# SS2D scan: VectorE instead of GpSimd makes the fourth product u in groups 3 and 6 of a step

## The chip, the cores and the metric

The kernel runs on one core of one Trainium2 chip. Its engines are TensorE (PE; its weight loads are listed as PEld), VectorE (DVE), ScalarE (ACT), GpSimd (POOL) and SyncE (SP), which issues the DMAs. Each engine works through its own queue in order; semaphores hold an instruction until what it needs is there. The metric is the device time of one execution in microseconds (us), lower is better.

## The reference, cut to what matters

The network has four layers on 8 images of 56 x 56 positions with 128 channels. Layers 0, 2 and 3 are deformable convolutions; layer 1 is a visual state space block (VSS), and the change lies in its scan ("SS2D"). Cut to that:

```python
xb = silu(dwconv3x3(in_proj(layer_norm(x))) + conv_b)         # 256 channels
xs = [x0, x1, reversed x0, reversed x1]                        # rows, columns, both ways
dts, B, C = split(x_proj_k @ xs_k)                             # for each direction k
dt = softplus(dt_proj_k @ dts + dt_bias_k)
def step(h, t):                                                # over the 3136 positions
    h = h * exp(dt_t * A) + (dt_t * u_t) * B_t                 # 256 channels x 16 states
    y = sum_n(h * C_t)
y = sum over the 4 directions of (y_k + Ds * xs_k)
x = x + out_proj(layer_norm(y) * silu(z));  x = x + mlp(layer_norm(x))
```

The state h has 256 x 16 = 4096 rows for each direction. The scan is linear in h, and the same for all rows, so that rows can stand in the 128 partitions and positions along the free axis.

## The kernel before, in words

The function `scans` of class `Vss` runs 128 *steps*: 8 images x 4 directions (in the order 1, 3, 0, 2) x 4 chunks of 784 positions. A step has 32 *units*: 8 *groups* cg of 32 channels, and in each group 4 scans sg of 4 states; a unit is 128 rows (32 channels x 4 states) x 784 positions. "Scan 3.2" is here scan sg=2 of group cg=3. For each unit:

- ScalarE makes dA = exp(A dt) into PSUM (`decay`, L1369; two buffers), so dA of a unit waits for the scan two units before.
- The product u = (dt x) B is made (`inputs`). For scans 0, 1 and 2 of a group VectorE makes it (L1379) from dtu, a copy of dt x in PSUM, and b; the tile u has two buffers. For scan 3 GpSimd makes it (L1375) from dt in SBUF and b; the tile is called up and has one buffer. GpSimd cannot read PSUM.
- VectorE scans (L1471): h = dA * h + u along the positions; h has three buffers, so a scan waits for the hc of three units before. ScalarE keeps the last column in st (L1474).
- GpSimd multiplies hc = h C (L1476); six buffers.
- TensorE adds hc over the states into acc (`add_sums`, L1401, two units at a time); ScalarE copies acc out after two groups (`close_sums`, L1412).

dtu of a group is a product of dt with the identity on TensorE (`spread`, L1363; four matmul rows, one buffer, so the spread of the next group waits for the last u that reads this one). dt of a group is fetched two groups ahead by SP (`fetch_dt`, L1314), b and c rows near the end of a step (`fetch_row`, L1307).

Beside this, `prepare` makes dt, dt x, B and C of the next step in pieces, one piece in each of scans 1 and 2 of every group. Its pieces for GpSimd are a sum (L1294) and a product (L1296) for each half of the channels; by program order they fall into groups 3 and 6. An output stage (layer norm, gate, projection, MLP; L1194 to L1252) and the next image's input stage (layer norm, 3x3 convolution as nine matmuls, SiLU) run as tasks that `advance` takes one piece of in scans 1, 2 and 3 of a group. The MLP takes fc1 (L1235), its bias on ScalarE (L1236), a Gelu (L1238) with a table load ahead of it and one back to the exp table (L1240), and fc2 with its bias row (L298, L1245, L1247).

Program order is not queue order. Every `tile` belongs to a pool with a number of buffers, and a scheduler sets the order of each engine's queue at build time: it takes instructions by priority (program order) as its own estimate of times makes them ready. So an instruction that becomes ready earlier or later in that estimate can move on its queue past others of independent work.

Of the kernel before, what the change touches and what calls it, by code (L numbers as in the profile page):

```python
# [133 lines left out]
NCG, NSG = DI // TC, NST // TS  # L134
# [855 lines left out]
class Vss:  # L990
# [332 lines left out]
    def scans(self):  # L1323
# [5 lines left out]
        order = [(cg, sg) for cg in range(NCG) for sg in range(NSG)]  # L1329
# [23 lines left out]

        def on_pool(t):

            return order[t][1] == NSG - 1

        def spread(at, t):

# [11 lines left out]
        def inputs(at, t):  # L1371
            s, (cg, sg) = state[at], order[t]
            if on_pool(t):
                u = self.work.tile([128, SC], F32, name="up", tag="up", bufs=1)
                nc.gpsimd.tensor_mul(u, s["dt", cg][:, 1], s["b", sg])  # L1375
            else:
                u = self.work.tile([128, SC], F32, name="u", tag="u", bufs=2)
                halves = [v.rearrange("p (x e) -> p x e", x=2) for v in (u, s["b", sg])]
                nc.vector.tensor_mul(halves[0], s["dtu", cg][:, :, :SH], halves[1])  # L1379
            s["u", t] = u  # L1380
# [47 lines left out]
        for now, (at, t) in enumerate(units):  # L1428
# [28 lines left out]
            if now + 1 < len(units):  # L1457
                decay(*units[now + 1])
                if not on_pool(units[now + 1][1]):
                    inputs(*units[now + 1])  # L1460

                if sg == NSG - 3 and now + 3 < len(units):
                    spread(*units[now + 3])
            if now + 2 < len(units) and on_pool(units[now + 2][1]):
                inputs(*units[now + 2])
# [100 lines left out]
```

## Time and profile before

| what | value |
|---|---|
| times of three runs | 18138.38, 18144.38, 18144.70 us (median 18144.38) |
| profiled execution | 18131.72 us |
| its span, first to last instruction | 18130.2 us, mean granted TensorE clock 0.849 |
| DVE, POOL, ACT, PE busy | 15374.0, 11790.9, 10917.1, 13876.0 us |
| scans, L1471, from u and from up | 3072 of 1838 ns, 1024 of 1833 ns |
| u on VectorE, L1379 | 3072 of 955 ns |
| up on GpSimd, L1375 | 1024 of 1860 ns |
| hc on GpSimd, L1476 | 4096 of 1877 ns |
| sum and product of the preparation, L1294, L1296 | 254 each in the scan stage, of 1862 and 2055 ns |
| spread, L1363 | 4096 matmul rows of 622 ns, four to a spread |

Busy time counts an instruction from its start to its end; neighbours on one engine overlap by some 0.1 us, so that the distance from start to start is a little shorter than the duration (two u in a row take 1.83 us). "Idle before, releaser" is the time that an engine stood still ahead of an instruction and what ended it. A wait view sums these by waiting line and releaser. In the timeline, equal neighbours stand in one row with their count.

### The profile page before, as it was taken

Reading aid. Unit: us, or ns where it says so; the run is one execution under the profiler, and the core shown is the slowest. Engines: PE = TensorE matmul, PEld = TensorE weight load, DVE = VectorE, ACT = ScalarE, POOL = GpSimd, SP = SyncE. Lnnn points to the kernel's source line nnn. Section 1 sums busy time; section 2 is a strip of 40 time slices with the busy share of each in tenths; the row PEclk is TensorE's granted clock in tenths of the full one; section 3 lists DMA queues with packets and bytes.
Section 4 is the critical chain, followed back from the end, with each engine's and each line's share of the span. In section 5 each row is a group of like instructions: output and inputs, shape, how many; then the busy total and the mean of one; then the engine's idle time right before and its main releaser. Section 6 shows DMA issues by size and latency. Waiting matters only on the chain. (4 is left out here: it accounts for less than half of the span.)

```text
span 18130.2 us, 255599 instructions
## 1 busy us (share of the span) xinstructions
PE 13876.0 (77%) x90059; PEld 6901.9 (38%) x90059; DVE 15374.0 (85%) x17784; ACT 10917.1 (60%) x19602; POOL 11790.9 (65%) x6462
## 2 busy tenths in 40 slices
PE   5777787688688688688788778778676888577777
PEld 4655422233232232232223223222134666455555
DVE  8888368998998998998998898899976887688886
ACT  4666555566566566566566566656554666456666
POOL 2221079998998998998998998999971111222221
PEclk7778888899899899899899899889886888677777
DMA  7777444444443443444443444444335777577777
GB/s 216 210 200 206 133 146 157 160 170 154 146 158 139 143 160 137 147 157 142 141 159 139 148 156 141 143 156 149 138 120 141 198 199 197 148 203 202 203 200 174
DMA packets 1341766, 2961.81 MB, mean 163 GB/s; under 512 B 91168, under 2 KB 892132, under 8 KB 1325836
## 3 DMA queue, kind: packets, MB, share of 16 engines
q1 hardware_dynamic: 1340460, 2945.21, 52.4%
q8 instruction: 720, 11.80, 0.3%
q14 instruction: 586, 4.80, 0.1%
HBM read 2243.88 MB, written 866.92 MB: 172 GB/s over the span
## 5 line engine op out<-in xcount | busy, mean ns | idle before, releaser
L1476 POOL TENSOR_TENSOR hc<-h,c 128x784 f32<-128x784 f32 x4096 | 7559.1, 1877 | 594.7 <-DVE h L1471 348.4
L1471 DVE TENSOR_TENSOR_SCAN h<-dA,st,u 128x784 f32<-128x784 f32 x3072 | 5572.7, 1838 | 367.1 <-ACT dA L1369 190.2
L1369 ACT ACTIVATE dA<-dt,v_A 128x784 f32<-128x784 f32 x4096 | 3743.1, 915 | 864.5 <-DVE h L1471 852.9
L1401 PE MATMUL acc<-hc,v_sum 128*32 128x392 f32 x16384 | 3105.8, 533 | 141.4 <-POOL hc L1476 139.8
L1379 DVE TENSOR_TENSOR u<-dtu,b 128x784 f32<-128x784 f32 x3072 | 2860.7, 955 | 398.8 <-PE dtu L1363 390.7
L1363 PE MATMUL dtu<-dt,ident 128*128 128x392 f32 x4096 | 2012.8, 622 | 1221.8 <-issue 864.5
L736 POOL TENSOR_TENSOR ay<-hat,om 112x756 f32<-112x756 f32 (+2 forms) x192 | 516.2, 2688 | 2755.4 <-ACT hat L727 2359.4
L1471 DVE TENSOR_TENSOR_SCAN h<-dA,st,up 128x784 f32<-128x784 f32 x1024 | 1877.2, 1833 | 297.0 <-POOL hc L1476 278.1
L1375 POOL TENSOR_TENSOR up<-dt,b 128x784 f32<-128x784 f32 x1024 | 1904.6, 1860 | 65.9 <-DVE h L1471 33.4
L807 ACT COPY st<-pt 128x448 f32<-128x448 f32 (+1 forms) x2240 | 1175.8, 541 | 1218.2 <-PE pt L805 1211.3
L1474 ACT COPY st<-h 128x1 f32<-128x1 f32 x3072 | 583.5, 190 | 2047.5 <-DVE h L1471 2040.5
L775 DVE TENSOR_TENSOR win<-win,patch 112x252 f32 (+2 forms) x3456 | 1691.7, 502 | 125.8 <-DVE win L775 33.1
L805 PE MATMUL pt<-ident,sw 112*128 112x112 f32 (+2 forms) x8960 | 1609.8, 310 | 208.2 <-DMA sw<-skew 208.1
L1401 PEld LDWEIGHTS acc<-hc,v_sum 128*32 128x32 f32 x16384 | 758.1, 115 | 2547.2 <-issue 1630.8
L1363 PEld LDWEIGHTS dtu<-dt,ident 128*128 128x128 f32 x4096 | 848.3, 227 | 2251.6 <-issue 1348.9
L766 POOL MEMSET win<- 128x1820 f32 (+2 forms) x384 | 630.4, 1648 | 1461.4 <-DMA skew<-win 1156.3
L821 PE MATMUL yps<-st,xw 128*32 128x48 f32 (+5 forms) x35840 | 1076.4, 245 | 399.1 <-ACT st L807 396.3
L805 PEld LDWEIGHTS pt<-ident,sw 112*128 112x128 f32 (+2 forms) x8960 | 1119.5, 161 | 493.3 <-DMA sw<-skew 169.7
L772 DVE TENSOR_TENSOR patch<-ay,hat 112x756 f32<-112x756 f32 (+2 forms) x1152 | 1222.1, 1066 | 20.9 <-POOL ay L736 17.9
L821 PEld LDWEIGHTS yps<-st,xw 128*32 128x32 f32 (+2 forms) x35840 | 755.4, 125 | 827.2 <-ACT st L807 475.9
L725 ACT ACTIVATE hat<-om,taps 112x252 f32<-112x252 f32 x1280 | 755.7, 729 | 287.5 <-DVE patch L772 270.2
L1128 PE MATMUL misc<-xn,v_tap 128*128 128x448 f32 x2016 | 837.4, 563 | 64.0 <-ACT xn L1162 27.2
(193 smaller groups left out, 19611.3 us busy)
## 6 DMA issues: line engine op xcount, KB each, us to landing
dt<-dds SPq DMA_DIRECT2D x1024, 784.0 KB
b<-rows SPq DMA_DIRECT2D x512, 392.0 KB
c<-rows SPq DMA_DIRECT2D x512, 392.0 KB
dds<-dd SPq DMA_DIRECT2D x256, 784.0 KB
sw<-skew SPq DMA_DIRECT2D x224, 812.0 KB
sw<-skew SPq DMA_DIRECT2D x224, 672.0 KB
sw<-skew SPq DMA_DIRECT2D x224, 588.0 KB
xw<-table SPq DMA_DIRECT2D x224, 320.0 KB
```

Source lines behind the costliest of these rows:

```text
L772: nc.vector.tensor_mul(patch[:n], bcast(a, 3, KX), bcast(b, 2, KY))
L775: self.last_add = nc.vector.tensor_add(to, to, patch[:n, NCB * p : NCB * (p + 1)]).ins
L805: last = nc.tensor.transpose(ps[:m, n * g : n * (g + 1)], sw[:n, g, p : p + m], self.net.ident[:n, :n])
L807: nc.scalar.copy(st[:m], ps[:m, : G * n])
L821: self.nc.tensor.matmul(yps[CG * g : CG * (g + 1), t0:t1], lhsT=xw[:m, k + part, CG * g : CG * (g + 1)], rhs=st[:m, at + t0 : at + t1], st ...
L1363: last = nc.tensor.matmul(ps[:, b, :SH], lhsT=self.net.ident, rhs=s["dt", cg][:, 1, SH * b : SH * (b + 1)], start=True, stop=True)
L1369: nc.scalar.activation(da[:, :SC], s["dt", cg][:, 0], AF.Exp, scale=w["A"][:, k, NSG * cg + sg : NSG * cg + sg + 1])
L1375: nc.gpsimd.tensor_mul(u, s["dt", cg][:, 1], s["b", sg])
L1379: nc.vector.tensor_mul(halves[0], s["dtu", cg][:, :, :SH], halves[1])
L1401: nc.tensor.matmul(acc[r : r + TC, :SH], lhsT=w["sum"], rhs=hc[:, SH * b : SH * (b + 1)], start=False, stop=sg == NSG - 1)
L1471: nc.vector.tensor_tensor_scan(hh[:, ::step], dA[:, :SC][:, ::step], u[:, ::step], st[:, t : t + 1], ALU.mult, ALU.add)
L1476: nc.gpsimd.tensor_mul(hc, hh, s["c", sg])
```

## The change: which u GpSimd makes

In groups 3 and 6 VectorE makes all four products u, scan 3 included, from dtu; there GpSimd makes none. In the other six groups nothing is different: scan 3's product is GpSimd's. So 256 of the 1024 up become u (2 in each of 128 steps), and the scans 3.3 and 6.3 read u instead of up.

```diff
         def on_pool(t):
 
-            return order[t][1] == NSG - 1
+            cg, sg = order[t]
+            return sg == NSG - 1 and cg not in (3, 6)
```

`on_pool` is asked in `inputs`, and in the loop over units: up is asked for two units ahead of its scan (L1464 to L1465), u one unit ahead (L1459 to L1460). The spread of the next group stands in the program after the u of scan 2 and, in groups 3 and 6 of the changed kernel, ahead of the u of scan 3; since both use the one buffer of dtu, that spread waits for this u.

## The prediction

> **What bounds the kernel now.** First the page: VectorE (DVE) is busy 85% of the span, GpSimd (POOL) 65%, but the page's slices show that GpSimd does nearly all of its work in the stage where both stand at 8 to 9 tenths, the SS2D scans. The first scan starts at 2363 us, the last ends at 13501 us: 128 steps, 11138 us, 87.0 us a step. All that the change touches lies in there.
>
> ```profile
> span 18130.2 us, 255599 instructions
> PE 13876.0 (77%) x90059; PEld 6901.9 (38%) x90059; DVE 15374.0 (85%) x17784; ACT 10917.1 (60%) x19602; POOL 11790.9 (65%) x6462
> ```
>
> Second, busy time by stretch, for three single steps. The columns are length, then busy time of PE, PEld, DVE, ACT, POOL, and the granted clock.
>
> ```profile
> 4815.53:4894.19 78.66, 41.76 (x176) 13.53 (x176) 77.60 (x57) 36.17 (x72) 73.22 (x42) 0.80 0.36 131
> 3831.00:3916.28 85.28, 73.68 (x277) 27.46 (x276) 79.61 (x58) 57.45 (x106) 82.32 (x46) 0.94 0.48 166
> 6047.60:6134.00 86.40, 60.48 (x205) 17.88 (x204) 78.43 (x58) 49.08 (x96) 86.40 (x48) 0.84 0.40 141
> ```
>
> The first step has none of the preparation on GpSimd: VectorE is never idle, and 78.7 us is its own work (32 scans, 24 products u). The second is the usual step with preparation; in the third GpSimd is busy all the time. So VectorE bounds, and what a step has over 78.7 is waits and a little stage work.
>
> Third, the waits of VectorE in the scan stage (waiting instruction, what it waited for, us in total, times, longest):
>
> ```profile
> DVE h L1471 <- POOL hc L1476: 341.2, 287, 3.3
> DVE u L1379 <- PE dtu L1363: 310.1, 130, 9.3
> DVE h L1471 <- ACT dA L1369: 195.5, 188, 5.0
> ```
>
> Placed by group and scan (group cg, scan sg), the 341 us lie: 72.3 at scan 3.3 and 72.2 at 6.3, the two that the change is about; the rest, by whole group 4, 5, 7, 0 and others, 54.4, 36.4, 72.4, 23.7 and about 10.
>
> Fourth, the timeline of group 3 in the step at 3831, VectorE and then GpSimd:
>
> ```profile
> 3863.30 0.97 DVE L1379 TENSOR_TENSOR u<-dtu,b 128x784 f32<-128x784 f32 x1
> 3864.19 3.58 DVE L1471 TENSOR_TENSOR_SCAN h<-dA,st,u 128x784 f32<-128x784 f32 x2
> 3869.69 1.85 DVE L1471 TENSOR_TENSOR_SCAN h<-dA,st,up 128x784 f32<-128x784 f32 x1 [1.92 <-POOL hc L1476]
> ```
>
> ```profile
> 3861.78 1.86 POOL L1375 TENSOR_TENSOR up<-dt,b 128x784 f32<-128x784 f32 x1
> 3863.59 1.89 POOL L1294 TENSOR_TENSOR dd<-dd,sp 128x784 f32<-128x784 f32 x1
> 3865.55 2.26 POOL L1296 TENSOR_TENSOR dd<-dd,xb 128x784 f32<-128x784 f32 x1
> 3867.76 7.38 POOL L1476 TENSOR_TENSOR hc<-h,c 128x784 f32<-128x784 f32 x4
> ```
>
> GpSimd runs product, sum and product in one piece before the first hc of the group. Three h buffers let scan 3.3 start only when hc 3.0 is done (3869.6): VectorE waits 1.92 us.
>
> **The change part by part.** (1) VectorE gets 256 more u (2 in each of 128 steps). Two u in a row take 1.83 us including overlap, one costs the queue 0.88: 256 x 0.875 = **+224 us**.
>
> (2) At 3.3 and 6.3 the new u runs inside the old wait. Wait by wait, the smaller of 0.875 and the wait adds to 45.2 + 46.4 = **-92 us**. The other waits right around them (a spread that TensorE delivers late for its own reasons, a late dA) hide more of it: counted the same way over scans 3.2 to 4.1 and 6.2 to 7.1, the cover is 80.7 + 63.4 = 144, so **-52 us** more. If that cover is gone, these 52 come back.
>
> (3) GpSimd loses 256 up of 1.86 us, but not where the text says. In the order of the built program, the place ahead of the sum and the product in group 3 is taken by group 4's up (it needs only dt, b and the single up buffer, and with up 3 gone that is free), and in group 6 by group 7's. The run of three before hc 3.0 stays, and the relief comes one group later. So scan 3.3 starts when it did. What can go is the hc waits of groups 4, 5, 7 and 0 and the rest at 6.3: 54.4 + 36.4 + 72.4 + 23.7 + 25.8 = 213. Bounds 0 and -213. I take rather over half, **-120**: in steps like the third above, where GpSimd is never idle, 48 operations become 45 and waits remain only around the runs of three. The early up 4 also wants dt 4 sooner: its 784 KB were issued at 3857.1, and at the 166 GB/s of that stretch take 4.7 us, about when up 4 would start (3861.8). A later landing would hold hc 3.0 behind it.
>
> (4) The spread (dtu, one buffer) of group 4 now waits for u 3.3 instead of u 3.2, so on TensorE's queue everything behind it (the sums over hc of groups 3) comes after that. What it costs VectorE depends on how many scans stand between the last u of a group and the first of the next. Over the whole stage, before: 0 scans 21 times, 1 scan 15, 2 or 3 scans 980; after: 50, 136 and 830. Prices from the trace: with 0 scans the gap is 2.79 us on average, as here:
>
> ```profile
> 4510.16 0.95 DVE L1379 TENSOR_TENSOR u<-dtu,b 128x784 f32<-128x784 f32 x1
> 4514.20 0.97 DVE L1379 TENSOR_TENSOR u<-dtu,b 128x784 f32<-128x784 f32 x1 [3.09 <-PE dtu L1363]
> ```
>
> with 1 scan 0.64 (16 places), with 2 scans 0.26. The 13 zeros at group 3 go, with the 41.4 us that stand at scan 3.2 for dtu: **-38**. The 121 new ones cost between 0 (a spread of 1.58 fits in a scan of 1.75) and 0.64 each, 77; the new ones stand mostly in steps with an undisturbed TensorE, so **+30**.
>
> (5) The 44 new zeros all stand at the end of a step, in the steps that run an output stage. There TensorE's queue changes: in 45 steps the next step's spread comes after the bias and first fc2 products, which need the Gelu; before, in none. And ScalarE now makes dA 7.2 after the Gelu and its two table loads. Rows of before:
>
> ```profile
> 3910.49 0.57 ACT L1236 ACTIVATE pre<-misc,v_col 128x392 f32<-128x392 f32 x1
> 3911.08 1.28 ACT L1238 ACT_TABLE_LOAD   x1
> 3912.37 1.51 ACT L1238 ACTIVATE pre<-pre 128x1568 f32<-128x1568 f32 x1
> ```
>
> ```profile
> 3910.43 1.58 PE L1363 MATMUL dtu<-dt,ident 128*128 128x392 f32 x4 [0.31 <-DVE u L1379]
> 3913.39 1.09 PE L298 MATMUL misc<-v_fc_b,ones 1*98 1x512 f32 x2
> ```
>
> From the start of scan 6.3: scan 1.85, st and dA 7.1 to 3.0, two copies of acc (0.90 each) to 4.8, the new acc 1.64 and sums 1.51 to 7.9 (the Gelu is done at 8.2, beside them), bias 1.09, x 0.3, fc2 0.5, spread 1.58: 11.4. Then u, two scans, u: next step's first scan at 16.7, where before it was 13.35 later (3902.93 to 3916.28): 3.35 more. In the steps of direction 2 the copies take 0.48 and acc 0.88, so 1.85. Mean 2.6 x 45 = **+117**; bounds 0 (the chain runs out early behind GpSimd's lead) and 45 x 3.35 = 150. The 44 further table loads of 1.28 us that ScalarE gets lie in this chain's shadow: 0, or up to 56 if not.
>
> SP's queue gets no other transfers, only some in another order: 0. TensorE and ScalarE compute the same: 0.
>
> Sum: 224 - 92 - 52 - 120 - 38 + 30 + 117 = **+69 us** on the profiled execution's 18131.7 (span 18130.2): 18201. The median of the three times, 18144.4, stands 12.7 higher: **18213 us**, 0.4% slower.
>
> One rule speaks against the change: the Trainium skill, Perfetto Trace Analysis, Identifying the Most-Contended Engine, says to improve the engine with the highest occupancy first. That would be VectorE, 77.60 of 78.66 us in the first stretch, and the change gives it more work: by the rule alone +224 us. The waits in the other two stretches say that part of this is hidden.
>
> **The rivals.** *Faster*: GpSimd's relief works in full, and the chain at the step's end is half hidden because GpSimd no longer lags there. 224 - 144 - 213 - 38 + 58 = -113: 18031. For it: the third stretch, where GpSimd is the bound outright. Against it: the run of three stays, and in the first stretch there is nothing to win. It decides if the hc waits fall below some 130 of 341 us. *Same*: relief a little larger than taken (-170) and the chain at 1.9 us (+85): -13, inside 0.2% (36 us), which is about what a measurement tells from no change. *The change does not do what it says*: the run of three keeps its length and relief is nil: 224 - 144 - 38 + 30 + 117 = +189: 18333. *Much slower*: nothing hides but the 92, all order costs at their top: 224 - 92 - 38 + 77 + 150 = +321: 18465.
>
> **How the numbers follow.** Forecast (from +36 to +190) 0.43, no relief or much slower 0.12, same 0.2, faster 0.25. So slower 0.55. The range leaves out a tenth at each end: below the faster rival's 18031 nearly, 18040, and above the no-relief case, 18335. The forecast's own range is 18180 to 18335.
>
> **What would show it.** Scans with u 3328, with up 768; the waits for hc at 3.3 fall by 0.9 each and do not vanish, those of groups 4, 5 and 7 shrink; waits of u for dtu grow at the end of 45 steps by some 2 us and vanish after u 3.2; the step without preparation takes 80.4 instead of 78.7. Wrong, if hc waits fall below 130 us (faster) or if u 0.0 after an output stage waits less than 1 us.

## The result, and the profile after

The changed kernel takes 18207.03 us (median of 7 runs, 18197.98 to 18216.24) where the kernel before takes 18144.70 on the same chip (7 runs, 18136.20 to 18157.83): ratio 1.0035, 95% interval 1.0026 to 1.0044. It is slower by 62 us; 18213 was predicted.

From the page of the changed kernel, span and busy time of each engine:

```profile
span 18205.5 us, 255708 instructions
PE 13892.2 (76%) x90059; PEld 6916.9 (38%) x90059; DVE 15561.4 (85%) x18040; ACT 11000.5 (60%) x19646; POOL 11341.0 (62%) x6206
```

DVE has 256 instructions more and POOL 256 fewer, as the change says. ACT has 44 more: all are table loads. The scan stage (start of the first scan to end of the last) went from 11137.8 to 11204.1 us, +66.3; what lies before and behind it differs by 0.6 and 8.4 us. So the loss is in the scan stage.

Busy time by stretch of the changed kernel, the same three steps as shown for before (columns: length, busy time of PE, PEld, DVE, ACT, POOL, granted clock, DMA share, GB/s):

```profile
4816.35:4896.33 79.98, 43.45 (x176) 13.99 (x176) 79.18 (x59) 36.16 (x72) 69.61 (x40) 0.81 0.36 126
3835.58:3924.40 88.82, 74.43 (x277) 27.42 (x276) 81.15 (x61) 59.34 (x106) 79.22 (x44) 0.92 0.48 162
6059.72:6144.11 84.39, 57.06 (x208) 17.79 (x208) 79.72 (x59) 51.81 (x100) 83.41 (x47) 0.84 0.43 155
```

Three kinds of step, three outcomes. The step without preparation went from 78.66 to 79.98: two u more, no wait to hide them. The step with preparation that ends in an output stage went from 85.28 to 88.82. The step in which GpSimd was busy without a break went from 86.40 to 84.39: there the change does what it looks like.

The waits of VectorE in the scan stage (waiting instruction, what it waited for, us in total, times, longest):

```profile
DVE u L1380 <- PE dtu L1364: 419.8, 213, 7.6
DVE h L1472 <- ACT dA L1370: 249.7, 179, 5.0
DVE h L1472 <- POOL hc L1477: 97.4, 128, 5.0
```

Before, these were 310.1 (dtu), 195.5 (dA) and 341.2 (hc). The wait for GpSimd fell by 244 us, more than the 212 (92 + 120) that the prediction took; the waits for TensorE and ScalarE rose by 110 and 54. Added up over the trace by place, the largest changes are (us, before to after): hc at scan 3.3, 72.3 to 5.2; at 7.3, 61.7 to 0; at 6.3, 72.2 to 26.9; dA at 3.2, 3.0 to 40.3; dtu for the u that stands right ahead of scan 7.2, 0 to 123.6; dtu for the u ahead of 7.0, 0 to 58.0; dtu ahead of 3.2, 41.4 to 0.

The 123.6 us are the end of the step. Timeline of VectorE, TensorE and ScalarE there, changed kernel (start us, duration, engine, line, operation, in square brackets the idle time before):

```profile
3914.56 0.95 DVE L1380 TENSOR_TENSOR u<-dtu,b 128x784 f32<-128x784 f32 x1
3919.14 0.97 DVE L1380 TENSOR_TENSOR u<-dtu,b 128x784 f32<-128x784 f32 x1 [3.64 <-PE dtu L1364]
3920.04 1.84 DVE L1472 TENSOR_TENSOR_SCAN h<-dA,st,u 128x784 f32<-128x784 f32 x1
```

```profile
3915.87 1.09 PE L298 MATMUL misc<-v_fc_b,ones 1*98 1x512 f32 x2
3916.89 0.46 PE L1245 MATMUL misc<-ident,x 128*98 128x128 f32 x2
3917.19 0.60 PE L1247 MATMUL misc<-v_fc,pre 128*98 128x128 f32 x4
3917.63 1.48 PE L1364 MATMUL dtu<-dt,ident 128*128 128x392 f32 x4
```

```profile
3913.44 1.28 ACT L1238 ACT_TABLE_LOAD   x1
3914.73 1.51 ACT L1238 ACTIVATE pre<-pre 128x1568 f32<-128x1568 f32 x1
3916.33 1.28 ACT L1370 ACT_TABLE_LOAD   x1
3917.62 0.92 ACT L1370 ACTIVATE dA<-dt,v_A 128x784 f32<-128x784 f32 x1
```

The u at 3914.56 is 7.2; it frees dtu at 3915.5. The next step's first spread could run then, but on TensorE's queue the bias, the first product of x and the first four rows of fc2 stand ahead of it, and fc2 reads what the Gelu makes. Here they put the spread off by 1.76 us (3915.87 to 3917.63). The u at 3919.14 is the next step's u 0.0, which stands ahead of scan 7.2 on VectorE's queue, so scans 7.2 and 7.3 wait with it. The last two ScalarE rows are the extra table load and the dA that needs it. From the start of scan 6.3 (3906.65) to the next step's first scan (3924.40) it is 17.75 us; before it was 13.35, predicted was 16.7.

### The profile page after: what moved, and what is told of

Read it like the earlier page. It is cut to its first block, busy times and chain, and to the rows that moved or that the text cites. A ratio compares the mean times of both kernels' runs of the same rounds, so it can differ in the third digit from the quotient of the medians.

```text
span 18205.5 us, 255708 instructions
## 1 busy us (share of the span) xinstructions
PE 13892.2 (76%) x90059; PEld 6916.9 (38%) x90059; DVE 15561.4 (85%) x18040; ACT 11000.5 (60%) x19646; POOL 11341.0 (62%) x6206
## 5 line engine op out<-in xcount | busy, mean ns | idle before, releaser
L1472 DVE TENSOR_TENSOR_SCAN h<-dA,st,u 128x784 f32<-128x784 f32 x3328 | 6029.7, 1837 | 409.0 <-ACT dA L1370 247.6
L1380 DVE TENSOR_TENSOR u<-dtu,b 128x784 f32<-128x784 f32 x3328 | 3093.4, 955 | 505.6 <-PE dtu L1364 500.5
L1402 PE MATMUL acc<-hc,v_sum 128*32 128x392 f32 x16384 | 2998.5, 538 | 24.8 <-POOL hc L1477 24.4
L1376 POOL TENSOR_TENSOR up<-dt,b 128x784 f32<-128x784 f32 x768 | 1424.4, 1855 | 51.8 <-DVE h L1472 48.8
L1472 DVE TENSOR_TENSOR_SCAN h<-dA,st,up 128x784 f32<-128x784 f32 x768 | 1403.1, 1827 | 31.0 <-POOL hc L1477 28.0
```

What stands on the lines that cost most here:

```text
L1402: nc.tensor.matmul(acc[r : r + TC, :SH], lhsT=w["sum"], rhs=hc[:, SH * b : SH * (b + 1)], start=False, stop=sg == NSG - 1)
L1472: nc.vector.tensor_tensor_scan(hh[:, ::step], dA[:, :SC][:, ::step], u[:, ::step], st[:, t : t + 1], ALU.mult, ALU.add)
```

## The experiments

All are measured against the same kernel before. Beside only3, only6, fix_pe and fix_all it took 18127.19 us (16 runs, 18118.21 to 18146.56), beside fix_first, relief, load and at15 18132.73 (19 runs, 18112.46 to 18144.08), beside only5 and at35 18129.82 (9 runs, 18105.83 to 18154.17). "Stage" is the change of the scan stage against the first profile of before. The table holds what the text below refers to: the change in each group, from scan 0 of the group to scan 0 of the next, summed over all 128 steps (us, added up from the traces).

| kernel | u on VectorE in groups | ratio | stage | group 0 | 1 | 2 | 3 | 4 | 5 | 6 | 7 |
|---|---|---|---|---|---|---|---|---|---|---|---|
| changed | 3, 6 | 1.0035 | +66 | -53 | -54 | +16 | +19 | -12 | -34 | +108 | +76 |
| only3 | 3 | 0.9987 | -40 | -6 | +7 | -3 | +33 | -7 | -10 | -36 | -19 |
| only6 | 6 | 1.0051 | +83 | -49 | -24 | +22 | -18 | +12 | -58 | +117 | +80 |
| fix_pe | 3, 6 | 1.0096 | +164 | -51 | +137 | +14 | +33 | -22 | -92 | +114 | +32 |
| fix_all | 3, 6 | 1.0033 | +52 | -54 | +98 | +17 | +22 | -26 | -71 | +110 | -43 |
| fix_first | 3, 6 | 0.9981 | -33 | -54 | -14 | +13 | +17 | -14 | -53 | +111 | -39 |
| at15 | 1, 5 | 0.9976 | -37 | -19 | +48 | +11 | -36 | +8 | +57 | -60 | -45 |
| only5 | 5 | 0.9955 | -91 | -22 | -26 | +16 | -11 | +9 | +51 | -61 | -47 |
| at35 | 3, 5 | 0.9951 | -95 | -12 | -30 | +9 | +16 | -7 | +59 | -81 | -49 |

### One group at a time

```diff
-            return sg == NSG - 1 and cg not in (3, 6)
+            return sg == NSG - 1 and cg not in (3,)      # only3
+            return sg == NSG - 1 and cg not in (6,)      # only6
```

> VectorE makes the fourth product in group 3 alone; group 6 is as before. The queues at the step's end stay as before: the next step's spread stands ahead of fc2 in all steps but one, and ScalarE has the table loads of before. Theory (the loss sits at the step's end, in the 45 steps whose spread comes after fc2): 128 u at 0.68 us are +87, the waits for hc at scan 3.3 (72) and for dtu at scan 3.2 (41) go, some new waits for dA come (+40): about 30 us faster than before, 18115. Rival (VectorE is saturated, every u costs): half of the changed kernel's loss or more, 18175 to 18230.

> VectorE makes the fourth product in group 6 alone. Here the order at the step's end changes as in the changed kernel (39 steps with fc2 ahead of the next spread, 44 more table loads). Theory: +87 for the u, -45 at scan 6.3 and -60 in group 7 for hc, +110 at scan 7.2 for dtu: slower than before by 70 to 110 us, 18215 to 18255, and with the loss of group 3 alone it adds up to the changed kernel's. Rival (every u costs alike): the same as with group 3 alone.

Measured: only3 18106.95 us (18096.12 to 18117.60), ratio 0.9987 [0.9978, 0.9996]; only6 18226.33, ratio 1.0051 [1.0037, 1.0064]. Both are what the theory said, and neither is what the rival said. The two differ by 119 us with the same number of products moved. In only6 TensorE's queue has the fc2 products ahead of the next step's spread in 39 steps and ScalarE has the 44 further table loads; in only3 the order is that of before in all but one step and there are no further loads. In only6, dtu ahead of scan 7.2 grows by 105.7 us; in only3 nothing is lost there. So the change in group 3 alone pays for itself, and the loss comes with group 6. -40 and +83 make +43 of the changed kernel's +66.

### Holding the order at the step's end

`issue_after(x)` lets the scheduler place an instruction only behind x on its queue. The first kernel holds the bias and all of fc2 behind the newest spread on TensorE. The second adds two holds: the Gelu behind the newest dA on ScalarE, and a group's first u behind the newest scan on VectorE. The third has these two, but holds only the bias, and with it what follows at once. The lines that note the newest dA and scan are left out here.

```diff
 # fix_pe
-        self.net.bias_row(po, n, w["fc2_b"], T)
+        with self.tc.issue_after(self.last_spread):
+            self.net.bias_row(po, n, w["fc2_b"], T)
         for t in range(T):
+          with self.tc.issue_after(self.last_spread):
             nc.tensor.matmul(po[:n, 128 * t : 128 * (t + 1)], lhsT=x[:, n * t : n * (t + 1)], rhs=self.net.ident, start=False, stop=False)
...
 # fix_all: fix_pe, and
+        with self.tc.issue_after(self.last_decay):
             last = nc.scalar.activation(pre, pre, AF.Gelu_apprx_tanh)
...
+                with self.tc.issue_after(self.last_scan) if sg == 0 and self.last_scan is not None else nullcontext():
                     nc.vector.tensor_mul(halves[0], s["dtu", cg][:, :, :SH], halves[1])
...
 # fix_first: fix_all without the hold inside "for t in range(T)"
```

> The changed kernel, with fc2 and its bias held behind the last spread on TensorE's queue; VectorE's and ScalarE's queues as in the changed kernel. Theory: the u after scan 7.1 waits for a spread alone (1.7 us) instead of 2.8 to 3.7, but scan 7.2 then waits for its dA behind the Gelu and the table loads: part of the loss comes back, 20 to 65 us of the changed kernel's 18207, so 18142 to 18187. Rival (the loss is VectorE's added work): no change from 18207.

> The changed kernel, with fc2 behind the last spread on TensorE, the Gelu behind the last dA on ScalarE, and a group's first u behind the last scan on VectorE: the step's end stands as before the change. Theory: the 124 us of waits for dtu at scan 7.2 go and nearly nothing takes their place: 100 to 130 us less than the changed kernel, 18077 to 18107, and so about 50 us faster than before. Rival (the loss is VectorE's added work): it stays within 20 us of 18207.

Measured: fix_pe 18310.23 us, ratio 1.0096 [1.0080, 1.0111]; fix_all 18189.72, ratio 1.0033 [1.0020, 1.0045]. Both miss their ranges. By the table group 7 did what was expected: +76 fell to +32 with TensorE's order and to -43 with all three. But group 1, which nobody had in mind, went from -54 to +137 and +98. TensorE and VectorE there, fix_pe:

```profile
3934.79 2.95 PE L1366 MATMUL dtu<-dt,ident 128*128 128x392 f32 x4 [3.84 <-issue]
3937.53 0.63 PE L1247 MATMUL misc<-ident,x 128*98 128x128 f32 x2
...
3942.83 2.33 PE L1276 MATMUL misc<-xb,v_xproj 128*40 128x392 f32 x3
...
3952.45 1.58 PE L1366 MATMUL dtu<-dt,ident 128*128 128x392 f32 x4
```

```profile
3954.08 1.85 DVE L1382 TENSOR_TENSOR u<-dtu,b 128x784 f32<-128x784 f32 x2 [3.52 <-PE dtu L1366]
```

The second half of fc2 asks for its hold later than the first, when "the newest spread" is already that of group 1. So it comes after that spread (3934.79), although TensorE stood idle for 3.84 us before it, and pushes the projection (L1276) back, and with it the spread of group 2 (3952.45). The u of group 2 waits 3.52 us in this step. Over the stage the wait for dtu at scan 2.0 was 84 us before and is 214 in fix_pe and 196 in fix_all, 130 and 112 more. The repair had the fault that it was to mend: an instruction held in front of a spread. The kernel without the second hold:

> The changed kernel, with only the bias and the first half of fc2 held behind the last spread, the Gelu behind the last dA, a group's first u behind the last scan. The run before this one held the second half too, behind a later spread, and lost 110 us to dtu at the first u of group 2, while group 7 gained 119 us on the changed kernel. Theory: group 7 keeps that, and group 1 and 2 go back to the changed kernel's: 18207 - 119 = 18088, about 60 us faster than before. Rival (what goes at the step's end always comes back elsewhere, since VectorE is saturated): within 30 us of 18207.

Measured: 18096.54 us (18092.84 to 18118.10), ratio 0.9981 [0.9972, 0.9990]. The same 256 u, the same relief of GpSimd, and 0.54% between the ratios of this and the changed kernel, some 98 us; by the stage 99. TensorE in fix_first at the end of the same step:

```profile
3902.69 1.58 PE L1366 MATMUL dtu<-dt,ident 128*128 128x392 f32 x4
3904.20 1.51 PE L1405 MATMUL acc<-hc,v_sum 128*32 128x392 f32 x8
3905.64 1.09 PE L298 MATMUL misc<-v_fc_b,ones 1*98 1x512 f32 x2
```

Spread first, bias 2.95 us later, and u 0.0 waits for nothing. That shows the cause of the loss: the order at the step's end. The hold on u covers the first u of every group, not only that of the next step; but by the table the gain lies in group 7 (+76 to -39), and group 1 gives 40 back. Of the three orders only TensorE's was held alone (fix_pe); what the other two cost apart was not tried. Group 6 costs as much as before the repair (+111): its own u, and the waits for dtu ahead of 7.0 (62 us), stay. Why the scheduler's estimate tips over with group 6 and not with group 3 was not tried.

### Relief and load by themselves

> Scans 3.3 and 6.3 have no product of their own: they read scan 2's u again (part of the computation is left out). GpSimd is relieved of the same 256 products as in the changed kernel and VectorE has the load of before. It shows the largest gain that relieving GpSimd can give: Theory: the waits for hc fall from 341 to about 130 us, 200 us less than before, 17930 to 17960. Rival (GpSimd's burst of three stays, so that the waits at 3.3 and 6.3 stay): 100 us less or smaller.

```diff
+            if cg in (3, 6) and sg == NSG - 1:
+                s["u", t] = self.kept  # scan 3 reads scan 2's u once more
+                return
```

The output of layer 1 is then another, and layers 2 and 3 take a slower way of fetching their samples, seen on the page of relief in a row that the page of before does not have:

```profile
L443 POOL DMA_INDIRECT sam<-patches,idx x7200 | 7163.4, 995 | 3386.9 <-issue 2153.1
```

So the total (30489 us) says nothing of the change, and only the scan stage, which comes before those layers, is read: 11006.6 us, -131. Expected was -200. Waits for hc fell from 341 to 192 and no further: at 3.3 by 29.5 and at 6.3 by 24.4, to some 43 and 48 each. That is the run of three on GpSimd, which does not go away when up 3 and up 6 go: an up, the sum and the product stand ahead of hc 3.0 in 44 steps (37 before) and ahead of hc 6.0 in 51 (50 before). In the changed kernel the same two places fell to 5.2 and 26.9; the rest, by the difference of the two kernels, is filled by the u that VectorE now makes there. But relief is not relief alone: its ScalarE, too, has the 44 further table loads at the step's end, and VectorE waits 38.6 us for ScalarE's copies into st at scan 7.3, where before it waited for none. So -131 is not the most that the relief could give. VectorE and GpSimd in group 3 of the changed kernel:

```profile
3871.47 0.95 DVE L1380 TENSOR_TENSOR u<-dtu,b 128x784 f32<-128x784 f32 x1
3872.34 0.96 DVE L1203 TENSOR_TENSOR yc<-yc,misc 128x784 f32<-128x784 f32 x1
3873.43 1.85 DVE L1472 TENSOR_TENSOR_SCAN h<-dA,st,u 128x784 f32<-128x784 f32 x1
```

```profile
3865.56 1.85 POOL L1376 TENSOR_TENSOR up<-dt,b 128x784 f32<-128x784 f32 x1
3867.37 1.88 POOL L1294 TENSOR_TENSOR dd<-dd,sp 128x784 f32<-128x784 f32 x1
3869.33 2.24 POOL L1296 TENSOR_TENSOR dd<-dd,xb 128x784 f32<-128x784 f32 x1
3871.52 5.55 POOL L1477 TENSOR_TENSOR hc<-h,c 128x784 f32<-128x784 f32 x3
```

up (now that of group 4), sum, product, hc: the run stands as predicted. hc 3.0 ends at 3873.4, and scan 3.3 starts then; until then VectorE makes u 3.3 and, in this kind of step, the output stage's product yc. Before, yc stood behind scan 3.3 (3869.69 to 3871.54):

```profile
3871.45 0.94 DVE L1203 TENSOR_TENSOR yc<-yc,misc 128x784 f32<-128x784 f32 x1
```

The wait is filled, not removed.

> VectorE makes the fourth u in groups 3 and 6 as in the changed kernel, and GpSimd still makes up there, which nobody reads. The load on VectorE without the relief. Theory: 256 u at 0.68 us are 175, of which some 90 to 140 lie in the old waits for hc and dtu, and the queues' order at the step's end costs up to 120: 60 to 160 us over before, 18205 to 18305, and with the relief's run it adds up to the changed kernel within 50 us. Rival (all of it is load, hidden nowhere): 175 us and more over before, 18320.

```diff
+            if sg == NSG - 1 and not on_pool(t):
+                up = self.work.tile([128, SC], F32, name="up", tag="up", bufs=1)
+                nc.gpsimd.tensor_mul(up, s["dt", cg][:, 1], s["b", sg])
```

Measured: 18405.05 us, ratio 1.0150 [1.0134, 1.0165], +272, far over the range. GpSimd and VectorE in group 6 of this kernel:

```profile
3932.17 1.83 POOL L1384 TENSOR_TENSOR up<-dt,b 128x784 f32<-128x784 f32 x1
3934.09 1.84 POOL L1376 TENSOR_TENSOR up<-dt,b 128x784 f32<-128x784 f32 x1
3935.88 1.84 POOL L1294 TENSOR_TENSOR dd<-dd,sp 128x784 f32<-128x784 f32 x1
3937.80 2.24 POOL L1296 TENSOR_TENSOR dd<-dd,xb 128x784 f32<-128x784 f32 x1
```

```profile
3941.93 1.85 DVE L1475 TENSOR_TENSOR_SCAN h<-dA,st,u 128x784 f32<-128x784 f32 x1 [2.50 <-POOL hc L1480]
```

Both products, the unread one and that of the next group, now stand ahead of the sum: a run of four. Waits for hc at 6.3 grew by 81 us, to 153, although a u now fills part of them. So the kernel does not isolate the load on VectorE, as it was meant to; it shows how dear one more operation in that run is. Nor do relief and load add up to the changed kernel, as was expected: by the stage -131 and +262 make +131, not +66.

### Other places for the same product

If it is the run that makes VectorE wait, what counts is whether taking a product from GpSimd breaks the run, and that need not be at the run's own place. The first of these kernels was made to ask whether the place matters at all; what it showed led to the other two.

```diff
-            return sg == NSG - 1 and cg not in (3, 6)
+            return sg == NSG - 1 and cg not in (1, 5)    # at15
+            return sg == NSG - 1 and cg not in (5,)      # only5
+            return sg == NSG - 1 and cg not in (3, 5)    # at35
```

> VectorE makes the fourth product in groups 1 and 5 instead of 3 and 6. The step's end keeps the order of before. Theory: in groups 1 and 5 there is little wait to fill (scan 1.3 has 5 us in all, 5.3 has 34), so the u cost 140 of their 175 us; GpSimd's relief reaches groups 2 and 6 and takes 60 to 120 us of hc waits: 20 to 80 us over before. Rival (the place does not matter, only GpSimd's total): within 20 us of the changed kernel without its loss at the step's end, 18090.

Measured: 18089.68 us (18085.58 to 18103.31), ratio 0.9976 [0.9966, 0.9986]. The theory as it stood then fell, and the rival's number (18090) was met. But the wait for hc at 6.3 was gone (-72.2), which a mere count of products does not explain. Two more kernels separate count and place:

> VectorE makes the fourth u in group 5 alone; GpSimd makes up in the other seven groups. With groups 1 and 5 the kernel took 0.9976 of before, and the 72 us that before waits for hc at scan 6.3 were gone, because up 6 moved out of the run up, sum, product ahead of hc 6.0 into the place of group 5's. At the step's end nothing changes. Theory (the gain comes from the run broken at group 6, group 1 only costs): 128 x 0.68 = 87 more for u, -72 at 6.3, -45 at 7.3 and -25 to -40 in the other hc and dtu waits: 18055 to 18085, at or below the kernel with groups 1 and 5; wait for hc at 6.3 near 0. Rival (only the number of products that GpSimd loses counts, not their place): as with group 3 alone, 0.9987, about 18107.

> VectorE makes the fourth u in groups 3 and 5; 256 more u as in the changed kernel, the order at the step's end as before the change. Theory (the places add up: group 3 alone gave -20 to -40, group 5 breaks the run at group 6): 18030 to 18070, the fastest so far; waits for hc below 120. Rival (only the number counts): as with groups 1 and 5, 18090. Second rival (what group 3's and group 5's relief fill are the same waits, so the second u of a step pays its full 0.68): the better of the two alone plus up to 50, 18100 to 18150.

Measured: only5 18047.23 us (18032.41 to 18052.72), ratio 0.9955 [0.9942, 0.9969]; at35 18039.04 (18032.24 to 18040.80), ratio 0.9951 [0.9937, 0.9964]. only5 came out 8 us below its range, and at35 inside its own. In only5 half as many products are moved as in at15, for twice the gain: the place decides, and the rival of at15 had met its number by chance. GpSimd in groups 5 and 6 of only5:

```profile
3885.61 5.53 POOL L1477 TENSOR_TENSOR hc<-h,c 128x784 f32<-128x784 f32 x3
3891.09 1.85 POOL L1294 TENSOR_TENSOR dd<-dd,sp 128x784 f32<-128x784 f32 x1
3892.89 1.85 POOL L1477 TENSOR_TENSOR hc<-h,c 128x784 f32<-128x784 f32 x1
3894.68 2.25 POOL L1296 TENSOR_TENSOR dd<-dd,xb 128x784 f32<-128x784 f32 x1
3896.87 7.36 POOL L1477 TENSOR_TENSOR hc<-h,c 128x784 f32<-128x784 f32 x4
```

With up 5 gone, up 6 moves a group forward, and the sum goes ahead of hc 5.3. Of the run of three, one operation is left between hc 5.3 and hc 6.0. The effect that hurt in the changed kernel (an up takes the place that came free) helps here. The waits of VectorE in only5:

```profile
DVE u L1380 <- PE dtu L1364: 381.8, 150, 80.8
DVE h L1472 <- POOL hc L1477: 205.4, 187, 3.2
DVE h L1472 <- ACT dA L1370: 190.4, 185, 5.0
```

(The 80.8 us is one wait ahead of the first scan; in the stage the dtu waits are 301.) hc fell by 136 us, 72.0 of them at 6.3 and 46.0 at 7.3, for 128 u at 0.66 us, 84; no other kind of wait grew by over 13. All waits of VectorE together fell by 175, which with the 84 gives the stage's -91. at35 removes the wait at 3.3 as well (-63.8), hc comes to 102, and the total is that of only5 within the scatter of the runs: what group 3 gives, its own 128 u take, nearly. The changes of only3 (-40) and only5 (-91) do not add up to at35's -95. So at35's range was met, but not for the reason given, that the places add up. It is faster than the kernel before and the changed one.

## Why the prediction was right, and where it was not

The direction and the size came as forecast: 18213 against 18207. Term by term, in us of the scan stage, waits from the sum over the trace:

| term of the prediction | predicted | measured |
|---|---|---|
| (1) 256 u on VectorE | +224 | +169 |
| (2) and (3) u in old waits, relief of GpSimd | -92 - 52 - 120 = -264 | -250 (hc -244, all other waits not named below together -6) |
| (4) spread at 3.2 | -38 | -41 |
| (4) spreads with one scan in between, now ahead of 7.0 | +30 | +58 (44 with one scan in between, 14 with two) |
| (5) end of the step | +117 | +124 |
| sum | +69 | +60, the stage +66 |

**(1) was mis-sized.** The prediction took half of a pair of u (1.83, less the overlap), 0.875, for each. The step without preparation, where VectorE waits for nothing, shows the price: 79.98 - 78.66 = 1.32 for two (80.4 - 78.7 was predicted), 0.66 each, 169 for 256. Over the whole stage, what is not wait grew by 176, 0.69 each. Why it is less than half a pair stands in the last section. This made the sum 55 too high.

**(2) and (3): the total was nearly right, its places were not.** The step that failed is "the run of three before hc 3.0 stays ... So scan 3.3 starts when it did". The run stays, as GpSimd's rows show, but the wait at 3.3 went nearly to zero instead of falling by 0.9 each time: relief shows that 29.5 of the 72.3 go with GpSimd's lighter load, and u 3.3 (with yc in some steps) fills the rest. The relief at 7.3 and the groups between came as said. (Of the third step's 48 operations on GpSimd two go, so 46 and not the 45 that the prediction names; its row now shows 47.) The other half failed in the opposite direction: the 52 us of other waits that were to hide u did not on balance go, since waits for dA grew by 54 (37 of it at scan 3.2, where the wait for dtu had gone by 41: what is late next).

**(4)** The 41 at 3.2 went. Of the new places with one scan between the last u and the next group's first, the 60 ahead of group 4 cost next to nothing and the 64 ahead of group 7 cost 44 us, 0.68 each, the upper price; with two scans in between another 14 came there. The spread ahead of 7.0 takes 2.82 us in the median, not the 1.58 that fits in a scan, and 40 of the 46 that were waited for with one scan in between stand right behind an fc1 product (L1235). The spread and the u 7.0 that waits for it, in the step shown above:

```profile
3906.43 2.82 PE L1364 MATMUL dtu<-dt,ident 128*128 128x392 f32 x4
3909.29 1.85 DVE L1380 TENSOR_TENSOR u<-dtu,b 128x784 f32<-128x784 f32 x2 [0.79 <-PE dtu L1364]
```

It took 2.82 before as well, but then, in all steps but one, two or more scans stood in between, and nothing of it was left as a wait. Why it is slower than others there was not tried.

**(5) was right and decided the sign.** 45 places, found from the order of the queues alone; 45 x 2.6 = 117 predicted, 124 measured (in 44 of them VectorE waited), and with the order held 98 of the loss came back. The single step was longer than worked out (17.75 against 16.7).

That the time came out within 6 us is in part luck: errors cancelled, -55 and -3 against +14, +28 and +7. With the -55 alone it would have been 18158, still inside the range of 18040 to 18335, but below the 18180 where the forecast's own range starts.

**The signs.** One of the two that were to prove it wrong came: hc waits below 130 (97) did not make the kernel faster, since the "Faster" rival also needed the chain at the step's end to be half hidden. The sign was badly chosen: the prediction's own terms already leave 129 of the 341 (92 and 120 less), and a wait that falls says nothing if another takes its place. The other, u 0.0 with less than 1 us of wait, did not come (2.8 on average). With that order held, fix_first has the chain gone altogether and is faster than before, at 0.9981 rather than the 0.994 of that rival.

On the rule that was weighed: VectorE was and is the busiest engine, and its own row in only5 shows DVE at 15465.6 us busy against 15374.0 before, in a shorter span. The Trainium skill, Perfetto Trace Analysis, Optimizing Scalar/DVE Operations, says that where VectorE is saturated, moving some work to ScalarE or GpSimd may make sense, and that between VectorE and GpSimd it might not help. Here the other direction gained 0.45% in only5. The same page's Optimization Strategy, to look for the gaps on the engine within the stretch and what ends them, agrees with this case: the 72.2 us at scan 6.3 were such a gap.

## What to carry to other kernels

An engine's total load is not what its neighbours wait for: look for the run of operations that stands ahead of the one they need, and take work away where the queue then breaks that run, which need not be where the run stands (0.9955 in group 5, 0.9987 in group 3, for the same 128 products). Where a scheduler orders the queues, compare the order of all of them before and after an edit, those of engines that the edit does not touch first: here fc2 slipped ahead of a spread in 45 steps, and that cost more than the edit's own balance gave. When such an order is held by hand, hold only the instruction that gets in the way; a hold on what follows moved the loss to another group.

## What was not expected of the hardware

A scan right behind the u that it reads starts 0.13 us after that u's end, and with another u in between it does not. VectorE of the changed kernel in a step without waits:

```profile
4845.85 3.58 DVE L1472 TENSOR_TENSOR_SCAN h<-dA,st,u 128x784 f32<-128x784 f32 x2
4849.35 1.83 DVE L1380 TENSOR_TENSOR u<-dtu,b 128x784 f32<-128x784 f32 x2
4851.10 1.84 DVE L1472 TENSOR_TENSOR_SCAN h<-dA,st,u 128x784 f32<-128x784 f32 x1
```

Two u take 1.75 us from start to the scan's start. A single one takes 1.08, as in fix_first:

```profile
3901.67 0.95 DVE L1383 TENSOR_TENSOR u<-dtu,b 128x784 f32<-128x784 f32 x1
3902.75 1.85 DVE L1476 TENSOR_TENSOR_SCAN h<-dA,st,u 128x784 f32<-128x784 f32 x1
```

So the second u costs 0.67: its own work less a gap that it fills. The spread of the same four matmul rows took 1.48 to 2.95 us in the rows above. The 8 us that the changed kernel is longer behind the scan stage have no cause that the runs show; they are within the scatter of one kernel's runs.
